# Re-pacing expert matmuls between the two halves of a macaron network, and rebuilding a state-space scan loop

## The chip, the cores and the metric

The kernel runs on one core of one Trainium2 chip. The metric is the device time of one execution in microseconds (us), the median of three runs. A core has TensorE (PE in the profile, with its weight loads as PEld), VectorE (DVE), ScalarE (ACT), GpSimd (POOL) and SyncE (SP); they run their own instruction streams and meet at semaphores.

## The reference

A batch of 8 sequences of 256 tokens, width 128, goes through four layers of the form "half a feed-forward, an attention, half a feed-forward", each on a layer-normed input. What matters here is layers 1 and 3:

```python
x = x + 0.5 * _L1_ffn_ref(_layernorm(x), ...)    # stage 3: 8 experts, a router, top 2
x = x + _L1_attn_ref(_layernorm(x), ...)         # stage 4: state-space scan, 16 states
x = x + 0.5 * _L1_ffn_ref(_layernorm(x), ...)    # stage 5
...
x = x + 0.5 * _L3_ffn_ref(_layernorm(x), ...)    # stages 9 and 11: attention, then 8 dense experts
x = x + _L3_attn_ref(_layernorm(x), ...)         # stage 10: selective scan, mlp, attention (gqa), mlp

# _L1_attn_ref, for each channel e and state n:
A = -exp(A_log);  a = exp(dt * A)
bt = where(abs(A) < 1e-5, dt, (a - 1) / (A + 1e-10))
h[t] = a[t-1] * h[t-1] + bt[t-1] * u[t-1]
y = sum over n of C[t, n] * h[t, n]
# _L1_ffn_ref
h = silu(xf @ gate_w + gate_b) * (xf @ up_w + up_b)
y = sum over the experts of probs[:, e] * (h @ down_w + down_b)
```

Stages 6 and 8 are a plain two-layer feed-forward (layer 2), stage 7 a chunked delta rule (l2_attn), and layer 0 (stages 0 to 2) an expert-choice mixture and an attention.

## The kernel before

All tokens go through stages 0 to 2. Then the tokens are split into two halves, a and b, of 4 sequences each (1024 tokens, 8 tiles of 128). Each half goes through stages 3 to 11; below "a7" is stage 7 of half a. Tokens lie on the partitions in the residual x; transposed copies (xnT) have the channels there.

`run` (L745) issues the stages in a written order: a3 a4 b3 b4 a5 a6 a7 b5 b6 b7 a8 a9 a10 b8 b9 b10 a11 b11. A scheduler then orders every engine's instructions; instructions issued earlier in the program go first where they are ready by its reckoning. So that the expert matmuls of one half fill the gaps of a dependent chain of the other, six pairs of stages are tied together by the dictionary `beside`: b3 to a4, a5 to b4, b5 to a7, a9 to b7, b9 to a10, a11 to b10. In the leading stage `step` (L790) notes certain matmuls: in l1_attn the two `cb` of each state (L996, 32 in all), in l2_attn the gram (L1117) and `ks` (L1188), in l3_attn the scan's `sc` (twice each, 64), the mlps' `ph` (8 each) and the `scT` of gqa (64). In the following stage `keep_pace` (L794) gives each expert matmul of fraction "part" of the stage an order-only dependency on the noted matmul at the same fraction of the list. It sets the place in TensorE's instruction stream and makes no semaphore wait.

The experts of l1_ffn (L822 to L914, stages 3 and 5) are 16 groups: 8 experts times two chunks of 512 tokens. A group has, for each of two blocks of 128 hidden units, `pg` (L895) and `pu` (L897), Silu on ScalarE (L899), the product on VectorE (L900), then `po` (L906), 8 matmuls of 128x128 into one PSUM tile, and four scalar_tensor_tensor on VectorE (L912), one for each tile of tokens, that add the tile times its router weight to x. The experts of l3_ffn (L1412 to L1438) are 16 groups as well: four `ph` (L1418), three activations and one VectorE operation into hT, 16 `po` (L1430), four scalar_tensor_tensor (L1436). Each float32 matmul stands in the profile as two records. An expert's weights come by a DMA into one of three buffers, issued by SyncE and ScalarE in turn.

l1_attn (L915 to L1011) has a prologue (norm, three projections `plow`, `pc`, `pdt` a chunk, softplus, causal convolution, Silu, and GpSimd copies that shift dt and u by one token), then a loop over 16 states. With all 1024 tokens of the half in a tile's free dimension, a state does:

- ScalarE: a = exp(A dt) (L983), th = tanh(A dt / 2) (L984), cu = dt u c2 (L985; c2 is 1 where |A| is tiny, else 0). exp and tanh of this loop, and the Silu of experts beside it, change the activation table.
- VectorE: th = (a + 1) th (L987), bu = th c1 us (L988)
- GpSimd: bu = bu + cu (L989)
- VectorE: four tensor_tensor_scan of 256 tokens, one for each sequence, with start value 0 (L992); then twice h = h cb (L997), where `cb` is C of this state spread over the partitions by a matmul (L996)
- TensorE: y += h, through the identity (L998)

The tiles at, bu, cu and h have two buffers each.

The steps of the prediction touch further: l2_attn's recurrence, 8 steps with VectorE, TensorE and GpSimd's diagonal products (`dg`, L1064, four a step); the batches of l3_scan (L1493): a convolution and transposes, eight `pbc` (L1564), eight steps of `sc` (L1570, one PSUM buffer), `gw` (L1576) and `y` (L1584), an output projection; l3_mlp (L1464) and l3_gqa (L1603).

## Time and profile before

| what | value |
|---|---|
| median of three runs | 3518.58 us (3516.72 to 3529.11) |
| the profiled execution | 3514.43 us |
| its span in the trace | 3512.2 us |
| mean TensorE clock granted | 0.815 of full speed |
| TensorE busy | 2757.2 us, 79% |
| VectorE, ScalarE, GpSimd busy | 51%, 28%, 14% |

The stages of the trace, in us from the start of the span, first instruction to last on any compute engine (a stage of one half overlaps its neighbour of the other):

| stages | from to |
|---|---|
| 0 to 2, all tokens | 0 to 963 |
| a3; a4 (its loop 1129 to 1262) | 963 to 1082; 1082 to 1268 |
| b3 (with and after a4) | to 1324 |
| b4 (its loop 1372 to 1507); a5 | 1324 to 1514; to 1570 |
| a6; a7 (its recurrence 1756 to 1816) | 1571 to 1600; 1571 to 1894 |
| b5; b6 | 1514 to 1889; 1891 to 1923 |
| b7; a8; a9 (experts from 2089) | 1889 to 2237; 1894 to 1957; 1957 to 2292 |
| b8; b9; a10 (scan, then gqa from about 2556) | to 2331; 2332 to 2805; 2303 to 2799 |
| a11 (experts from 2913); b10 (scan from 2845, gqa from about 3073) | 2800 to 3322; 2819 to 3315 |
| b11 | 3317 to 3508 |

How to read the profile: busy times are of one execution. A stage's limit is read from its own stretch, not from the totals: in some stretches TensorE is busy throughout, in others it waits for a chain of VectorE, ScalarE and GpSimd. A row of a table of stretches has the stretch, its length, then the busy time of PE, PEld, DVE, ACT and POOL with the number of instructions, the granted TensorE clock, and the DMA engines' share and rate. A row of groups has the line, engine, operation, tiles and shapes, how many, then busy us and the mean in ns, then the engine's idle time before them and what ended it.

### The profile page before, as it was taken

The page shows a single profiled execution, that of the slowest core. Times are in us where ns is not written, and L with a number is a line of the kernel's source. Part 1 is how long each engine was busy: PE and PEld are TensorE (multiplying, and loading weights), DVE is VectorE, ACT ScalarE, POOL GpSimd, SP SyncE. Part 2 cuts the span into 40 slices and gives each one's busy share as a digit, 9 for nine tenths or more (in the row PEclk, how much of TensorE's full clock was granted, in tenths as well). Part 3 has the DMA queues.
Part 4 walks back from the last instruction along what each step waited for, and adds up shares of the span by engine and source line. Part 5 has one row for each costly group of instructions (what it writes and reads, how often), then busy time and mean ns, then how long its engine had stood idle before and what let it go on. Part 6 is the DMA issues. An engine that isn't in the chain of part 4 may idle for free.

```text
span 3512.2 us, 38332 instructions
## 1 busy us (share of the span) xinstructions
PE 2757.2 (79%) x14748; PEld 1815.4 (52%) x14748; DVE 1798.2 (51%) x4474; ACT 993.2 (28%) x1497; POOL 505.9 (14%) x559
## 2 busy tenths in 40 slices
PE   5674687586396786797888888988959989849999
PEld 3463354355253342354664666655635556625666
DVE  5722454672346868766565655454463354443332
ACT  1010233101124625522233213342223332213322
POOL 0055110024201211301030112000020000120000
PEclk8587799668687987897788659988969969959969
DMA  5021433201200000011200300010021100110100
GB/s 196 7 32 26 109 85 116 82 20 23 56 23 3 10 28 3 9 32 49 76 7 15 102 12 13 19 41 1 21 67 28 50 3 7 34 51 26 35 12 25
DMA packets 103233, 136.18 MB, mean 39 GB/s; under 512 B 22933, under 2 KB 83546, under 8 KB 96922
## 3 DMA queue, kind: packets, MB, share of 16 engines
q1 hardware_dynamic: 67530, 85.61, 8.0%
q10 hardware_dynamic: 22848, 37.36, 3.4%
q0 software_dynamic: 12672, 10.76, 2.2%
q8 instruction: 116, 1.90, 0.2%
q14 instruction: 67, 0.55, 0.1%
HBM read 106.17 MB, written 27.53 MB: 38 GB/s over the span
## 4 chain that ended last, share of the span: by engine, by line
PE 46%; DVE 13%; ACT 4%; POOL 3%; issue 2%; DMA 1%; ACTq 0%; POOLq 0%; DVEq 0%; SPq 0%
PE ph L1418 6%; PE po L1430 6%; PE po L906 2%; PE fl L1136 2%; PE pbc L1564 2%; PE ctx L588 2%; DVE h L992 2%; POOL bu L989 2%; PE sc L1570 2%; PE pg L895 2%; PE pu L897 1%; PE y L1584 1%; PE tp L218 1%; PE po L1029 1%; PE sc L539 1%
## 5 line engine op out<-in xcount | busy, mean ns | idle before, releaser
L1430 PEld LDWEIGHTS po<-w_e,hT 128*128 128x128 f32 x2048 | 257.0, 193 | 73.6 <-issue 52.3
L1430 PE MATMUL po<-w_e,hT 128*128 128x128 f32 x2048 | 280.0, 281 | 7.9 <-DVE x_res L1436 4.2
L1418 PE MATMUL ph<-x2T,w_e 128*128 128x512 f32 x512 | 270.1, 632 | 10.0 <-ACT hT L1426 9.5
L1426 ACT ACTIVATE hT<-ph,w_l_cols 128x512 f32<-128x512 f32 x192 | 131.7, 687 | 292.2 <-PE ph L1418 291.6
L542 DVE TENSOR_REDUCE nm<-sc 128x3 f32<-128x384 f32 (+1 forms) x192 | 132.4, 690 | 150.5 <-PE sc L541 150.1
L906 PEld LDWEIGHTS po<-w_e,hT 128*128 128x128 f32 x1024 | 137.7, 203 | 99.9 <-DVE hT L900 51.2
L906 PE MATMUL po<-w_e,hT 128*128 128x128 f32 x1024 | 153.0, 295 | 28.6 <-DVE hT L900 15.3
L578 ACT ACTIVATE pr_e<-scT 128x384 f32<-128x384 f32 (+1 forms) x192 | 114.6, 597 | 192.6 <-PE scT L576 186.7
L218 PE MATMUL tp<-c_ident,xn 128*128 128x128 f32 x208 | 54.7, 399 | 144.3 <-DVE xn L238 137.9
L899 ACT ACTIVATE gs<-pg,w_l_bias 128x512 f32<-128x512 f32 x128 | 87.9, 687 | 263.4 <-PE pg L895 260.2
L998 PE MATMUL y<-h,c_ident 128*128 128x512 f32 x128 | 89.3, 836 | 89.2 <-DVE h L997 89.1
L895 PE MATMUL pg<-xnT,w_e 128*128 128x512 f32 x256 | 142.2, 639 | 9.0 <-ACT gs L899 9.0
L427 ACT ACTIVATE gs<-pg 128x512 f32<-128x512 f32 x64 | 38.2, 597 | 370.8 <-PE pg L422 370.8
L897 PE MATMUL pu<-xnT,w_e 128*128 128x512 f32 x256 | 140.8, 634 | 2.5 <-ACT gs L899 2.5
L432 PE MATMUL po<-w_l_wd,hT 128*128 128x128 f32 x512 | 84.4, 318 | 73.5 <-DVE hT L428 73.4
L1436 DVE SCALAR_TENSOR_TENSOR x_res<-po,gt,x_res 128x128 f32<-128x128 f32 x256 | 74.3, 347 | 120.6 <-PE po L1430 120.4
L912 DVE SCALAR_TENSOR_TENSOR x_res<-po,pr,x_res 128x128 f32<-128x128 f32 x256 | 75.0, 342 | 109.5 <-PE po L906 109.3
L539 PE MATMUL sc<-ks,qs 72*128 72x256 bf16 x256 | 79.8, 312 | 60.8 <-DVE nm L542 45.5
L1418 PEld LDWEIGHTS ph<-x2T,w_e 128*128 128x128 f32 x512 | 84.8, 197 | 81.2 <-ACT hT L1426 42.1
L440 POOL DMA_INDIRECT l_acc<-eo,idx x64 | 99.5, 1554 | 156.3 <-DMA l_acc<-eo,idx 67.2
L432 PEld LDWEIGHTS po<-w_l_wd,hT 128*128 128x128 f32 x512 | 76.7, 226 | 86.6 <-DVE hT L428 85.5
L588 PE MATMUL ctx<-pr_e,vz 128*32 128x256 f32 x512 | 116.9, 395 | 4.8 <-ACT pr_e L578 4.6
(578 smaller groups left out, 5934.2 us busy)
## 6 DMA issues: line engine op xcount, KB each, us to landing
l_parts<-sT SPq DMA_DIRECT2D x48, 192.0 KB
qs<-l_parts SPq DMA_DIRECT2D x16, 576.0 KB
w_l_wu<-in_l_wu ACTq DMA_DIRECT2D x8, 1024.0 KB
w_l_wg<-in_l_wg SPq DMA_DIRECT2D x8, 1024.0 KB
w_l_wd<-in_l_wd SPq DMA_DIRECT2D x8, 1024.0 KB
w_e<-in_l_e SPq DMA_DIRECT2D x16, 512.0 KB
w_e<-in_l_e ACTq DMA_DIRECT2D x16, 512.0 KB
w_e<-in_l_e ACTq DMA_DIRECT2D x16, 384.0 KB
```

The costliest lines, as they stand in the source:

```text
L432: nc.tensor.matmul(po[:, h, :], hT[:, k, h * P : (h + 1) * P], w["l0_wd"][:, e, k, :], start=(k == 0), stop=(k == 3),)
L440: nc.gpsimd.indirect_dma_start(out=acc[:, :], out_offset=bass.IndirectOffsetOnAxis(ap=idx[:, j : j + 1], axis=0), in_=eo[:, h, :], in_offs ...
L539: nc.tensor.matmul(sc[:, jj, 0:S], qs[0:72, h, 0:P], k, start=True, stop=False)
L542: nc.vector.tensor_reduce(blocks[:, hp * pr : hp * pr + hp, :], sc[:, :, 0:384].rearrange("p h (k t) -> p h k t", t=P), AX.X, ALU.max, neg ...
L578: nc.scalar.activation(pe, sc[:, :, 0:384], AF.Exp, scale=float(1.0 / np.sqrt(np.float32(8.0))))
L588: nc.tensor.matmul(o, z, pe[:, 0:S], start=(j == 0), stop=False)
L895: self.keep_pace(nc.tensor.matmul(pg, wg[:, c], xnT[:, cols], start=True, stop=True), (G * e + g) / (8 * G))
L897: self.keep_pace(nc.tensor.matmul(pu, wu[:, c], xnT[:, cols], start=True, stop=True), (G * e + g) / (8 * G))
L906: nc.tensor.matmul(po[:, i, :], hT[:, k, i * P : (i + 1) * P], wd[:, k * P : (k + 1) * P], start=(k == 0), stop=(k == 1),)
L1418: mm = nc.tensor.matmul(ps, we[:, k * P : (k + 1) * P], xnew[:, 512 * g : 512 * g + 512], start=True, stop=True)
L1426: nc.scalar.activation(hT[:, k, :], ps, AF.Relu, bias=bias)
L1430: nc.tensor.matmul(po[:, i, :], hT[:, k, i * P : (i + 1) * P], we[:, (4 + k) * P : (5 + k) * P], start=(k == 0), stop=(k == 3),)
```

## The change

There are four edits, in three places.

1. `beside` gets a stretch of the leading stage's list: the experts are spread over the fractions lo to hi of it. b3/a4, a5/b4 and a9/b7 keep 0 to 1; b5/a7 becomes 0 to 0.4, b9/a10 0 to 0.5, a11/b10 0.5 to 1.
2. l1_attn notes its two `pc` matmuls, in the prologue, four times each: 8 marks ahead of the 32 of the loop.
3. In l1_ffn the four scalar_tensor_tensor of a group become four ScalarE multiplications by the router weight into a new tile eo (two buffers) and one GpSimd addition of 128x512 into x.
4. In the scan loop the tile at holds two states, and the exponentials and tangents of two states are issued together; cu is made by a GpSimd tensor_scalar with one buffer in place of ScalarE; a GpSimd memset clears a at the first token of each sequence, and one recurrence over 1024 tokens takes the place of the four.

```diff
@@ run
-            beside = {(b, 3): (a, 4), (a, 5): (b, 4), (b, 5): (a, 7), (a, 9): (b, 7), (b, 9): (a, 10), (a, 11): (b, 10)}
+            beside = {
+                (b, 3): (a, 4, 0.0, 1.0), (a, 5): (b, 4, 0.0, 1.0), (b, 5): (a, 7, 0.0, 0.4), (a, 9): (b, 7, 0.0, 1.0),
+                (b, 9): (a, 10, 0.0, 0.5), (a, 11): (b, 10, 0.5, 1.0),
+            }
...
@@ keep_pace
-            mark = self.pace[int(part * len(self.pace))]
+            lo, hi, steps = self.pace
+            mark = steps[int((lo + (hi - lo) * part) * len(steps))]
@@ l1_ffn
+                    eo = wk.tile([P, 4, D], F32, name="eo", tag="eo")
                     for i in range(4):
-                        t = 4 * g + i
-                        nc.vector.scalar_tensor_tensor(
-                            self.x[:, t, :], po[:, i, :], pr[:, t, e : e + 1], self.x[:, t, :], ALU.mult, ALU.add
-                        )
+                        nc.scalar.mul(eo[:, i, :], po[:, i, :], pr[:, 4 * g + i, e : e + 1])
+                    xs = self.x[:, 4 * g : 4 * g + 4, :]
+                    nc.gpsimd.tensor_tensor(xs, xs, eo, ALU.add)
@@ l1_attn
-                    nc.tensor.matmul(ps, w["l1_in"][:, P + 64 : P + 80], xnT[:, c], start=True, stop=True)
+                    mm = nc.tensor.matmul(ps, w["l1_in"][:, P + 64 : P + 80], xnT[:, c], start=True, stop=True)
+                    self.step(mm, 4)
...
-                    at = wk.tile([P, 2, T], F32, name="at", tag="at")
-                    a, th = at[:, 0], at[:, 1]
-                    bu, cu, h = (wk.tile([P, T], F32, name=nm, tag=nm) for nm in ("bu", "cu", "h"))
-                    nc.scalar.activation(a, dts, AF.Exp, scale=A[:, n : n + 1])
-                    nc.scalar.activation(th, dts, AF.Tanh, scale=Ah[:, n : n + 1])
-                    nc.scalar.activation(cu, dtu, AF.Copy, scale=c2[:, n : n + 1])
+                    if n % 2 == 0:
+                        at = wk.tile([P, 2, 2, T], F32, name="at", tag="at")
+                        for i in range(2):
+                            nc.scalar.activation(at[:, i, 0], dts, AF.Exp, scale=A[:, n + i : n + i + 1])
+                            nc.scalar.activation(at[:, i, 1], dts, AF.Tanh, scale=Ah[:, n + i : n + i + 1])
+                    a, th = at[:, n % 2, 0], at[:, n % 2, 1]
+                    bu, h = (wk.tile([P, T], F32, name=nm, tag=nm) for nm in ("bu", "h"))
+                    cu = wk.tile([P, T], F32, name="cu", tag="cu", bufs=1)
+                    nc.gpsimd.tensor_scalar(cu, dtu, c2[:, n : n + 1], None, ALU.mult)
...
                     nc.gpsimd.tensor_tensor(bu, bu, cu, ALU.add)
-                    for b in range(self.B):
-                        s = slice(b * S, b * S + S)
-                        nc.vector.tensor_tensor_scan(h[:, s], a[:, s], bu[:, s], 0.0, ALU.mult, ALU.add)
+                    nc.gpsimd.memset(by_b(a)[:, :, 0:1], 0.0)
+                    nc.vector.tensor_tensor_scan(h, a, bu, 0.0, ALU.mult, ALU.add)
```

More of the change, by code (lines that the diff above doesn't have):

```diff
@@ L770, in run @@
                 if on(k):
-                    half.steps, half.pace = [], steps.get(beside.get((half, k)), [])
+                    other, stage, lo, hi = beside.get((half, k), (None, 0, 0, 0))
+                    half.steps, half.pace = [], None
+                    if (other, stage) in steps:
+                        half.pace = lo, hi, steps[other, stage]
                     half.stage(k)
@@ L787, in __init__ @@
         self.side, self.tag = ("left", "right")[k], "ab"[k]
-        self.steps, self.pace = [], []
+        self.steps, self.pace = [], None
     def step(self, inst, weight=1):
```

## The prediction

> **What bounds the kernel now.** I read the engine totals first, then the chain that ended last, then busy time by stage, then the scan loop instruction by instruction.

> ```profile
> PE 2757.2 (79%) x14748; PEld 1815.4 (52%) x14748; DVE 1798.2 (51%) x4474; ACT 993.2 (28%) x1497; POOL 505.9 (14%) x559
> ...
> PE 46%; DVE 13%; ACT 4%; POOL 3%; issue 2%; DMA 1%; ACTq 0%; POOLq 0%; DVEq 0%; SPq 0%
> ```

> TensorE is the common bound, but only 79% busy: the 21% is what re-pacing can win, if it lies where experts can be put. The table of stretches shows where (start and end, length, busy of PE, weight load, DVE, ACT, POOL, then the granted clock):

> ```profile
> 1129.00:1262.00 133.00, 98.91 (x215) 37.49 (x216) 107.37 (x147) 73.36 (x68) 41.65 (x16) 0.82 0.04 12
> 1262.00:1325.00 63.00, 62.96 (x311) 40.54 (x309) 38.50 (x103) 18.79 (x26) 0.00 (x0) 1.00 0.10 29
> ...
> 1816.00:1894.00 78.00, 52.25 (x161) 28.58 (x160) 54.19 (x102) 39.83 (x47) 2.16 (x2) 0.79 0.02 5
> ...
> 2556.00:2650.00 94.00, 57.22 (x314) 35.47 (x312) 51.21 (x128) 21.75 (x51) 21.96 (x61) 0.67 0.24 66
> ...
> 2990.00:3038.00 48.00, 47.32 (x303) 31.34 (x303) 21.48 (x41) 10.29 (x17) 3.21 (x3) 1.00 0.11 35
> ```

> Row 1 is half a's scan loop: TensorE idle a quarter, VectorE the longest. Row 2 is what b's experts of stage 3 have left after it: TensorE full. Row 3 is the end of a's l2_attn, row 4 the start of a's gqa (26 and 37 us idle). Row 5 is one of four batches of b's l3_scan with a's experts inside: TensorE full. The other loop, half b's (1372 to 1507), takes 135 us.

> Inside a scan loop VectorE and GpSimd take turns. Two places, each with what ran at the same moment (start, duration, engine):

> ```profile
> 1200.22 1.22 DVE L987 SCALAR_TENSOR_TENSOR at<-at 128x1024 f32<-128x1024 f32 x1
> ...
> 1203.44 2.35 POOL L989 TENSOR_TENSOR bu<-bu,cu 128x1024 f32<-128x1024 f32 x1 [6.78 <-ACT at L984]
> ...
> 1203.87 3.00 DVE L987 SCALAR_TENSOR_TENSOR at<-at 128x1024 f32<-128x1024 f32 x1
> ```

> The same instruction takes 1.22 us alone and 3.00 us when it starts 0.43 us into GpSimd's add: it ends 1.08 us after the add does, so it hardly ran beside it.

> [...] L997, one input in PSUM, keeps its 0.67. [...]a scan of 256 takes 0.71, four follow each other in 2.42. [...]

> **Part 1, the scan loop.** ScalarE's work (three 1.15 us activations a state and table loads) isn't the loop's limit; taking cu away and pairing exp and tanh frees it, and gains nothing by itself. What counts is the new GpSimd multiply: 128x1024 float32, one SBUF input, scalar per partition. No such operation is in the trace. Its neighbours are:

> ```profile
> L1108 POOL TENSOR_SCALAR bT<-bT 128x1024 f32<-128x1024 f32 x2 | 5.6, 2782 | 0.0
> ...
> L969 POOL COPY us<-u 128x1020 f32<-128x1020 f32 x2 | 2.1, 1034 | 251.9 <-ACT u L961 251.9
> ```

> I take 2.78, the same instruction with an immediate scalar, VectorE idle beside it; ends 1.03 (the copy) and 3.3 (softplus' blocked add, L704, 3.33). [...] 2.78 + 2.35 + L987 1.20 + L988 1.28 + the scan. The one scan costs 2.40 by the four's 2.42 less a little; the merge is worth almost nothing, and the memset (128x4; a 128x16 takes 153 ns) only writes and hides under other waits. Sum 10.0, with about 0.3 us of handovers 10.3 a state, 165 for 16 states, against 133 and 135: **+30 each, +60**. Queued behind the multiply on GpSimd is the same state's add, and behind that VectorE's scan; cu has one buffer, so multiply n+1 can start only after add n[...]. Ends: 1.03 gives 8.6 a state, +3 each; 3.3 gives +43 each; if the two engines ran freely together, VectorE's own 7.2 would give -17 each.

> **Part 2, stage 3 and 5 experts.** The order of the built instructions: before, 5 of 16 expert groups (one expert on 512 tokens) end beside the other half's l1_attn and 11 after it; changed, 3 stand in its prologue, 1 near its end, 12 after it, none in the loop. So the weighted pc marks pull experts ahead of the loop, into a place where TensorE is mostly idle. The 11 groups take row 2's 63 us at a full clock, 5.7 each; a twelfth is +5.7. Moving the combining step off VectorE (four of 0.34 us a group) to ScalarE (four of some 0.27, from the PSUM copy L659, at best) and one GpSimd add (1.04, the 128x512 of L1483) costs nothing under full TensorE: ScalarE's 2 x 0.69 + 4 x 0.3 = 2.6 of 5.7, and po, with its one buffer, is free after 1.2 us instead of 1.4. The experts' weight loads (one in three buffers, from SyncE's and ScalarE's queues in turn) move with the groups: a load has two experts, four groups or 23 us, of lead, and the DMA engines are 0.03 to 0.12 busy there, so I cost them at nothing; without that cover an expert would wait for its load at each e. The last group's chain gets some 1.5 longer, and three groups in the prologue with their Silu between the exponentials cost about 1 us of tables and queue. 5.7 + 1.5 + 1 = **+8 each, +16**; ends 0 and +14 each.

> **Part 3, a7 to a9.** In the new order b5's last groups stand before a7's end (before, three stood at its very end), so l2_ffn of b (b6, 24 us of TensorE) runs in row 3's 26 us of idle; a8 (27 us) goes behind b7's gram, into a stretch of 66 us with 17 idle, 9 of it usable. 24 + 9 = **-33**. a9's experts no longer go into b7's recurrence; its attention does (56 us of TensorE against about the same in experts before), so nothing else is won. Ends: 0, if a7's tail is held up by VectorE (54 of 78 busy), and -70, if most of the 121 us idle between 1571 and 2296 is filled.

> **Part 4, a10 with b9.** Before, eight expert groups were left for gqa and the mlp. Now 15 stand before 55% of a10's instructions, five of them in row 4's stretch: 5 x 7.3 = 36.5, just its 37 us idle. b10's norms then hide in a10's end, 6 us more: **-43**; ends -55 and -20.

> **Part 5, b10 with a11.** Groups now start at 0.5: after the scan. In the new order 8 of 16 stand beside b10's gqa and mlp, and 8 after b10's end. Beside the scan stand only a11's attention (batches 1 and 2) and nothing (3 and 4). Taking 8 groups out of row 5's kind of stretch looks like a gain of 58 us of TensorE. But a batch alone is a chain: convolution and transposes 8 us, 4 pbc 8, eight steps of sc 0.92, gw 0.96 and handovers at 2.2, the end 4: 38 us, TensorE busy 27 of it, at a lower clock (0.67 to 0.8 elsewhere at that busy share) some 46, against 48 now. So -4 for the two batches, the eight groups cost 8 x 7.3 = +58 after b10's end, the mlp is 7 shorter, b11's norms hide, 10: **+37**. If the lone scan goes at TensorE's pace: 0.

> **Sum.** +60 +16 -33 -43 +37 = +37. Against the profiled execution's 3514.4 (span 3512.2 and 2.2 around it) this is 3551; the median of the runs is 4.1 above that execution: **3555**.

> **Rivals.** R1, not slower: the GpSimd multiply is cheap, 1.03. The loop loses 3 each rather than 30, the sum becomes -17: 3502. It decides from 1.6 us down (37 over 32 states is 1.16 off 2.78). For it: the copy's row; against it: the same instruction type at 2.78. R2: b10's lone scan keeps TensorE's pace, part 5 is 0: 3519. [...] against it: sc has one buffer, and every step waits for gw. R3: GpSimd's queue. The new expert adds wait for ScalarE, which waits for TensorE, and l2_attn's diagonal products (L1064, 1.06 us, four of each 7.2 us step) stand behind them in order: two recurrences of 8 steps get one add (1.04) a step longer, +17, and b5's groups, held by the same queue, end as late as before, which takes half of part 3's gain, +17: 3589. For it: they share a queue; against it: few b5 groups stand in the recurrence. That the experts leave the scan loop instead of filling it is in the forecast already.

> **Chances.** Forecast 0.5, R1 0.2, R2 0.15, R3 0.15. A measurement of this kernel can tell about 0.5% from no change, 3501 to 3536. Half of R1 and the low end of part 3 are faster: 0.15. The rest of R1, R2 and a little of the forecast are same: 0.22. Slower: 0.63. Range 3497 (R1 and some of part 3's low end) to 3600 (R3, or a 3.3 us multiply).

> **What would show it.** In the loop: GpSimd's cu at 2.7 to 2.9 us, L987 and the scan lengthened or waiting for GpSimd, about 165 us a loop. 12 groups after each loop. b7's start near 1889 + 76 - 33. No idle stretch at gqa's start in a10. In b10 about 46 us for batches 3 and 4, and 58 us of experts alone between b10's end and b11. A multiply near 1 us, or batches of 35 us, would make the prediction wrong.

## The result, and the profile after

| | before | changed |
|---|---|---|
| median | 3519.32 us (4 runs, 3516.72 to 3529.11) | 3559.84 us (4 runs, 3551.65 to 3572.22) |
| ratio | | 1.0113, 95% interval 1.0073 to 1.0153 |
| span of the profiled execution | 3512.2 us | 3549.9 us |
| mean TensorE clock | 0.815 | 0.802 |

The change makes the kernel 1.1% slower. The forecast was 3555. The total is right and so is its sign; but the sum is right by luck: two of its terms are wrong by about 54 us in opposite directions, and that is the lesson of this case.

The engine totals of the changed kernel come first:

```profile
PE 2820.9 (79%) x14748; PEld 1845.6 (52%) x14748; DVE 1774.8 (50%) x4122; ACT 981.3 (28%) x1687; POOL 745.2 (21%) x687
```

TensorE issues the same 14748 records and is busy 64 us longer, at a mean clock of 0.802 where it was 0.815. So matmuls run slower somewhere: a hint at the clock that the totals before couldn't give. GpSimd is busy 239 us longer, with its waits inside instructions counted (4.88 us for a multiply of 2.65, below).

To find where the time went, I cut both traces at the same events: the last matmul of stage 2, of a5, of a9, the first `pv` of b10's scan, the last matmul of b11.

| section | before | changed | measured | forecast |
|---|---|---|---|---|
| up to the end of stage 2 (unchanged code) | 962.7 | 966.5 | +3.8 | 0 |
| stages 3 to 5 with both scans (parts 1, 2) | 606.8 | 628.6 | +21.8 | +76 |
| a6 to a9, b5 to b7 (part 3) | 721.4 | 741.2 | +19.8 | -33 |
| to b10's scan (part 4) | 554.8 | 504.0 | -50.8 | -43 |
| b10, a11, b11 (part 5) | 660.9 | 703.9 | +43.0 | +37 |
| sum | 3506.7 | 3544.3 | +37.6 | +37 |

The stretches of the changed kernel that answer to the rows shown of before (stretch, length, busy of PE, PEld, DVE, ACT and POOL, then the clock): a's scan loop, the experts after it, the end of a's l2_attn, the start of a's gqa, and batches 3 and 4 of b10's scan.

```profile
1130.00:1264.00 134.00, 111.13 (x126) 32.04 (x124) 115.93 (x80) 41.77 (x43) 120.12 (x49) 0.55 0.00 0
1264.00:1339.00 75.00, 75.00 (x347) 47.12 (x347) 29.40 (x59) 32.77 (x77) 15.31 (x12) 0.96 0.13 38
1838.00:1912.00 74.00, 48.01 (x182) 28.80 (x182) 53.92 (x125) 37.59 (x51) 3.43 (x3) 0.82 0.05 13
2600.00:2694.00 94.00, 84.23 (x513) 56.35 (x511) 57.82 (x147) 32.03 (x66) 21.46 (x60) 0.96 0.24 66
2934.00:3031.00 97.00, 69.41 (x406) 42.55 (x402) 34.64 (x53) 9.93 (x17) 5.02 (x4) 0.77 0.02 7
```

Row 1: the loop takes 134 us, not 165. GpSimd is busy 120 of them. TensorE has 126 records where it had 215 and yet is busy longer: with no experts in the loop the clock is 0.55, where it was 0.82 with them. Row 2: 12 groups after the loop and the rest of one that began in it, in 75 us. Row 3: a7's end has b6 in it and is 74 long, where it was 78. Row 4: the idle of gqa's start is filled, 84 of 94 busy where it was 57. Row 5: batches 3 and 4 without experts, with the 7 us ahead of them. From its first `pv` to its last matmul a batch takes 44.8 and 44.4 us; the same two took 43.6 and 44.8 before, with experts between (before's row of 48 us is wider than the batch in it).

**The scan loop.** Here is the part of its timeline that decides (start, duration, engine, line; in square brackets the idle time before):

```profile
1202.63 2.29 DVE L1004 TENSOR_TENSOR_SCAN h<-at,bu 128x1024 f32<-128x1024 f32 x1 [1.93 <-POOL bu L1001]
1202.69 4.88 POOL L997 TENSOR_SCALAR cu<-dtu,c 128x1024 f32<-128x1024 f32 x1
1204.84 2.07 DVE L999 SCALAR_TENSOR_TENSOR at<-at 128x1024 f32<-128x1024 f32 x1
...
1208.86 2.34 POOL L1001 TENSOR_TENSOR bu<-bu,cu 128x1024 f32<-128x1024 f32 x1 [1.24 <-DVE bu L1000]
1209.23 3.05 DVE L999 SCALAR_TENSOR_TENSOR at<-at 128x1024 f32<-128x1024 f32 x1
```

The multiply is recorded with 4.88 us, which looks like a disaster. But it starts just after the scan, waits for it until 1204.9, and then needs its 2.65. L999 starts at the same moment and takes 2.07, only 0.86 more than the 1.21 it takes alone: it ran **beside** most of the multiply. Against the two-input add, two lines down, it takes 3.05. So the add shuts VectorE out for nearly all its 2.34 us (0.37 had gone before L999 began, 1.84 it was delayed), the multiply for 0.86 of its 2.65.

**b7's recurrence.** Its first `ks` to its last took 54.5 us before and 103.5 after. Before, with a9's experts beside it:

```profile
2099.00:2120.00 21.00, 20.65 (x162) 18.38 (x161) 9.16 (x21) 2.59 (x5) 9.16 (x9) 1.00 0.01 2
2120.00:2140.00 20.00, 19.78 (x153) 17.44 (x153) 8.14 (x19) 2.86 (x6) 10.93 (x11) 1.00 0.10 27
2140.00:2158.00 18.00, 18.00 (x140) 16.07 (x140) 7.44 (x19) 2.77 (x7) 4.83 (x6) 1.00 0.01 1
```

And the same recurrence in the changed kernel, with a9's attention beside it:

```profile
2063.00:2090.00 27.00, 23.36 (x96) 21.60 (x96) 12.15 (x23) 3.74 (x9) 8.23 (x8) 0.50 0.00 1
2090.00:2118.00 28.00, 27.54 (x113) 24.92 (x112) 9.97 (x22) 2.69 (x8) 7.19 (x7) 0.50 0.00 1
2118.00:2146.00 28.00, 28.00 (x114) 25.01 (x113) 7.45 (x17) 1.27 (x4) 9.36 (x10) 0.50 0.00 1
2146.00:2173.00 27.00, 26.53 (x118) 25.10 (x117) 7.60 (x18) 1.78 (x5) 0.43 (x1) 0.50 0.00 1
```

In both TensorE is busy almost throughout. The clock column is what differs: 1.00 before, 0.50 changed. In 20 us it gets through 153 records before and about 80 after.

### The profile page after: what moved, and what is told of

It is laid out like the page before. It is cut to its first block, busy times and chain, and to the rows that moved or that the text cites. A ratio compares the mean times of both kernels' runs of the same rounds, so it can differ in the third digit from the quotient of the medians.

```text
span 3549.9 us, 38408 instructions
## 1 busy us (share of the span) xinstructions
PE 2820.9 (79%) x14748; PEld 1845.6 (52%) x14748; DVE 1774.8 (50%) x4122; ACT 981.3 (28%) x1687; POOL 745.2 (21%) x687
## 5 line engine op out<-in xcount | busy, mean ns | idle before, releaser
L1442 PE MATMUL po<-w_e,hT 128*128 128x128 f32 x2048 | 272.6, 280 | 7.9 <-DVE x_res L1424 4.6
L1430 PE MATMUL ph<-x2T,w_e 128*128 128x512 f32 x512 | 262.1, 617 | 9.2 <-ACT hT L1438 9.2
L908 DVE SCALAR_TENSOR_TENSOR hT<-pu,w_l_bias,gs 128x512 f32<-128x512 f32 x128 | 95.5, 746 | 165.6 <-PE pu L905 145.6
L914 PE MATMUL po<-w_e,hT 128*128 128x128 f32 x1024 | 147.5, 289 | 27.4 <-DVE sp L698 18.7
L1010 PE MATMUL y<-h,c_ident 128*128 128x512 f32 x128 | 115.0, 1026 | 55.1 <-DVE h L1009 55.1
L922 POOL TENSOR_TENSOR x_res<-x_res,eo 128x512 f32<-128x512 f32 x64 | 85.4, 1335 | 346.8 <-ACT eo L920 346.7
L997 POOL TENSOR_SCALAR cu<-dtu,c 128x1024 f32<-128x1024 f32 x32 | 155.2, 4851 | 4.1 <-DVE dtu L980 1.2
L218 PEld LDWEIGHTS tp<-c_ident,xn 128*128 128x128 f32 x208 | 35.5, 183 | 180.4 <-DVE xn L238 91.5
```

The lines of the kernel that those rows point to most:

```text
L914: nc.tensor.matmul(po[:, i, :], hT[:, k, i * P : (i + 1) * P], wd[:, k * P : (k + 1) * P], start=(k == 0), stop=(k == 1),)
L997: nc.gpsimd.tensor_scalar(cu, dtu, c2[:, n : n + 1], None, ALU.mult)
L1010: nc.tensor.matmul(y[:, s], self.ident, h[:, s], start=(n == 0), stop=(n == N - 1))
L1430: mm = nc.tensor.matmul(ps, we[:, k * P : (k + 1) * P], xnew[:, 512 * g : 512 * g + 512], start=True, stop=True)
L1442: nc.tensor.matmul(po[:, i, :], hT[:, k, i * P : (i + 1) * P], we[:, (4 + k) * P : (5 + k) * P], start=(k == 0), stop=(k == 3),)
```

## The experiments

A reader needs three columns for most of them: the time from stage 2's end to a5's end, from there to a9's end, and from there to the kernel's last matmul (before: 607, 721, 1216; changed: 629, 741, 1208). They are from one profiled execution each; the medians of before, measured alongside, were 3516.8 to 3518.9.

| kernel | median | ratio to before, 95% interval | sections |
|---|---|---|---|
| scan_alone | 3551.5 | 1.0120 (1.0064 to 1.0175) | 646, 722, 1210 |
| combine_alone | 3522.5 | 1.0021 (1.0003 to 1.0038) | 617, 712, 1220 |
| places_alone | 3516.4 | 0.9995 (0.9973 to 1.0017) | 575, 761, 1210 |
| cu_copy | 3552.1 | 1.0119 (1.0064 to 1.0174) | 622, 741, 1208 |
| cu_act | 3539.6 | 1.0071 (1.0047 to 1.0095) | 614, 749, 1210 |
| b5_full | 3536.3 | 1.0058 (1.0039 to 1.0077) | 631, 726, 1210 |
| a11_full | 3496.2 | 0.9942 (0.9922 to 0.9963) | 629, 745, 1149 |
| hold_attn | 3583.3 | one run | 631, 776, 1201 |
| dense_fill | 3533.8 | one run | 628, 750, 1189 |
| best1 | 3423.9 | 0.9735 (0.9710 to 0.9759) | 574, 732, 1164 |

### Each part alone

scan_alone is before.py with edit 4 (at, cu, memset, one recurrence) and nothing else.

> The kernel before with the scan edit alone (two states a tile, cu as a GpSimd tensor_scalar, one recurrence). In the built order 2 of 16 expert groups stand beside l1_attn, 14 after it (before: 5 and 11). Theory A (the forecast: the multiply shuts VectorE out for its whole 2.78 us): each loop 165 us instead of 133, and 3 more groups of 5.7 after it: 3519 + 60 + 34 = about 3613. Theory B (the multiply shuts VectorE out for under 1 us of it): each loop stays at 134, so only the groups count: 3519 + 34 + 2 = about 3555.

3551.5: theory B. Its loops are 134.2 and 132.5 us long (first L987 to the end of the last scan), before 132.0 and 134.1. All of its loss lies in the groups that follow each loop, 14 instead of 11: the loop is as long as before, but in the scheduler's order it has been emptied of experts. So the rewritten loop isn't free either: in before's first loop the experts held VectorE for 9.4 us (L900, L912), in this one's for 1.5, and the loop got no shorter by that.

places_alone has edits 1 and 2 (the stretches and the marks) and nothing else.

> The kernel before with the new stretches and the pc marks alone (scan and combining step as before). In the built order 9 of 16 groups stand beside l1_attn. If the old scan loop can carry 7 groups at little cost, 4 groups of 5.7 fewer follow each loop: -40 or so; the rest as in the changed kernel's trace: +18 in a7 to a9, -51 in a10, +43 in b10 and b11. Together 3519 - 40 + 10 = about 3490. If the loop grows by what it takes in (its VectorE is 107 of 133 us busy), about 3530.

The first section is 32 us shorter: the old loops take in 6 to 7 groups each, where they had 3 to 4, and get only 5 us (1130.8 to 1267.6) and 2 us longer. The late section is as expected. But a6 to a9 cost 40, not 18, so the whole comes out at zero where I expected -27. b7's recurrence takes 103 us, as in the changed kernel; the further 20 us lie ahead of a7's recurrence (9) and between b7's gram and its recurrence (10), and aren't explained.

combine_alone has edit 3 and nothing else.

> The kernel before with the combining step alone on ScalarE and GpSimd. Stages 3 to 5 end TensorE-bound as before, so nothing there. Theory E (rival R3 of the prediction, seen in b5_full's trace, where a7's recurrence with b5's groups in it took 74 us instead of 60): the GpSimd adds stand in one queue with the recurrence's diagonal products, +13 in a7's recurrence and none in b7's, which has l3 experts: 3517 + 13 = 3530. Without such a queue: 3517.

3522.5, and a7's recurrence takes 60 us as before. Theory E, and rival R3 of the prediction with it, fall: the GpSimd adds don't hold the recurrence. The edit isn't neutral everywhere: its loops take 138 us each, 6 and 4 more than before, and its second section is 9 shorter. What slowed a7's recurrence in b5_full is seen below.

### The multiply in the loop

cu_copy, on the changed kernel:

```diff
-                    nc.gpsimd.tensor_scalar(cu, dtu, c2[:, n : n + 1], None, ALU.mult)
+                    nc.gpsimd.tensor_copy(cu, dtu)
```

> The changed kernel with cu made by a GpSimd copy of dtu (the factor c2 is left out of the computation). A copy of this size took 1.03 us before. Theory A: each of 32 states gets 1.75 us shorter, 3560 - 56 = about 3504. Theory B: the copy shuts VectorE out about as long as the multiply does, and only every second state, in which the add waited for cu, gets 0.6 shorter: 3550 to 3560, the loops 129 to 134 us.

3552.1, loops of 130.0 and 128.9 us (134.0 and 132.9 in the changed kernel): theory B. Here is the copy, behind the scan as the multiply was:

```profile
1210.07 2.29 DVE L1004 TENSOR_TENSOR_SCAN h<-at,bu 128x1024 f32<-128x1024 f32 x1 [1.35 <-POOL bu L1001]
1210.09 3.09 POOL L997 COPY cu<-dtu 128x1024 f32<-128x1024 f32 x1
1212.27 1.99 DVE L999 SCALAR_TENSOR_TENSOR at<-at 128x1024 f32<-128x1024 f32 x1
```

The copy takes 0.8 us once the scan is over and delays L999 by 0.78, about as much as the multiply of 2.65 (0.86). How long a GpSimd instruction runs and how long it shuts VectorE out are two numbers. What sets the second isn't separated: the copy reads one input and shuts VectorE out for nearly all its time, the multiply reads one and doesn't.

cu_act takes the multiply off GpSimd again:

```diff
-                    nc.gpsimd.tensor_scalar(cu, dtu, c2[:, n : n + 1], None, ALU.mult)
+                    nc.scalar.activation(cu, dtu, AF.Copy, scale=c2[:, n : n + 1])
```

> The changed kernel with cu back on ScalarE (one buffer, otherwise as changed); the built order of the experts is the changed kernel's. Theory B (the multiply shuts VectorE out for about 0.86 us of its 2.7): each state gets that much shorter, 32 x 0.86 = 28: loops of 120 instead of 134 us, 3560 - 28 = about 3532. If the multiply costs the loop nothing at all: loops of 134 and 3560.

3539.6, between the two; neither expectation holds. The loops are 129 us, 4 to 5 shorter each, not 14. The trace shows where most of the rest went. L1009 is the product with `cb`, first in the changed kernel's loop, then in this one's:

```profile
L1009 DVE TENSOR_TENSOR h<-h,cb 128x512 f32<-128x512 f32 x30 | 19.7, 675 | 0.8 <-PE cb L1008 0.8
...
L1009 DVE TENSOR_TENSOR h<-h,cb 128x512 f32<-128x512 f32 x30 | 20.1, 679 | 13.8 <-PE cb L1008 13.8
```

VectorE's wait for GpSimd's add fell from 17.3 us to 6.4, but now it waits 13.8 us for TensorE, at a mean clock of 0.58 in a loop without experts. The total is weak evidence: the profiled execution, 3550.9, is one of the two longest of seven, and of the 15 us that its first section wins the second loses 8; what of the 15 lies outside the loops isn't explained.

### b7's recurrence and the clock

b5_full changes one number of the changed kernel, b5's stretch of a7, back to 0 to 1.

> The changed kernel with b5's experts again over all of a7, so that a9's experts again stand in b7's recurrence and a9's attention ahead of it. Theory C (the recurrence took 110 instead of 59 us in the changed kernel because it has a9's attention in it in place of experts, and TensorE's clock is 0.55): recurrence back at about 60 us, b7 starts later again by about 40, a9 ends some 18 us earlier: 3542. Rival D (it is slow because GpSimd's queue or the new combining step holds it): recurrence stays above 100 us and the later start adds to it: 3580 or more.

3536.3: theory C. b7's recurrence takes 54.5 us again. But a7's takes 73.6, which neither theory had. Its steps take 18.9, 14.1, 10.7 and then 7.1 to 7.7, and its eight `ks` 1.9, 1.75, 1.75 and then 0.98 us. At a clock of 0.50, in the changed kernel's b7, eight `ks` take 1.75: the start of a7's recurrence has that length too. best1 shows the clock itself there, 0.50, without the combining step (below). The kernel before has a slow start for one step only (`ks` of 1.9 us, a step of 14.9 at a mean clock of 0.60, from the next one on 1.00).

hold_attn and dense_fill ask whether it is the clock or the work in between. Both keep a9's attention out of b7's recurrence; dense_fill adds work.

```diff
# hold_attn: a9's first matmuls, in the order only, behind a late ks of b7
-                        nc.tensor.matmul(ps, w["l3_in"][:, j * P : (j + 1) * P], xnT[:, c], start=True, stop=True)
+                        mm = nc.tensor.matmul(ps, w["l3_in"][:, j * P : (j + 1) * P], xnT[:, c], start=True, stop=True)
+                        if self.pace and self.pace[0] == 0.0 and self.pace[1] == 1.0:
+                            self.keep_pace(mm, 0.999)
# dense_fill: behind ks, in each step of half b
+                        if self.tag == "b":
+                            fill = psum.tile([P, 512], F32, name="fill", tag="fill")
+                            for _ in range(3):
+                                nc.tensor.matmul(fill, self.ident, kd.rearrange("p b s -> p (b s)"), start=True, stop=True)
```

> The changed kernel with a9's attention held, in the order of TensorE's instructions, behind the seventh step of b7's recurrence, so that the first six or seven steps run with nothing between them. Theory F (TensorE's clock is low where it has only small matmuls, and the recurrence goes at that clock): the clock stays under 0.65 and a step takes 9 us or more, against 7.2 with experts beside it. Theory G (the steps are slow since a9's attention stands between them in order and waits): a step takes 7.2 us or less.

> The changed kernel with three extra matmuls of 128x512 in each step of b7's recurrence (their result is not used; a9's attention falls behind the recurrence in the built order, as in hold_attn). That is 2.8 us of TensorE a step at full clock. Theory F: they raise the clock to 0.85 or more, the step's own matmuls get faster, ks 1.2 us instead of 1.75, and a step takes no longer than in hold_attn, 7 to 9 us. Theory G: the clock stays and a step gets 3 to 5 us longer than in hold_attn.

Inside the recurrence of hold_attn, which has only its own matmuls of 32 columns:

```profile
2080.00:2105.00 25.00, 21.05 (x94) 20.39 (x94) 5.46 (x11) 0.53 (x2) 8.24 (x8) 0.50 0.00 1
2105.00:2130.00 25.00, 20.72 (x93) 19.92 (x92) 5.16 (x11) 0.80 (x3) 11.12 (x11) 0.50 0.00 1
```

And of dense_fill:

```profile
2020.00:2040.00 20.00, 19.06 (x121) 14.40 (x119) 7.22 (x14) 0.53 (x2) 14.08 (x13) 0.99 0.01 2
2040.00:2060.00 20.00, 20.00 (x128) 15.15 (x128) 5.27 (x15) 0.80 (x3) 12.23 (x12) 1.00 0.00 1
```

A step takes 11.0 us alone, and **7.1 us with three more matmuls in it**, whose result nobody uses; `ks` goes from 1.88 to 0.97. The first step of dense_fill takes 12.8, then the clock is at 0.99 to 1.00. Theory F's numbers hold in both runs: 0.50 and 11.0 us a step without the added matmuls, 0.99 to 1.00 and 7.1 with them. G has a share: with a9's attention in between, at the same 0.50, a step took 14.1 instead of 11.0. So of the 7 us that a step of the changed kernel lost, 4 are the clock's effect on the bare step and 3 the attention that stands in line at that clock. With the dead work the kernel takes 3533.8 us, against 3583.3 in hold_attn (one run each); 26 us of that lie between a5's end and a9's. Against the changed kernel's 3559.8 it is no proof: there the same stretch is 9 us shorter (741 against 750), since its attention needn't wait behind the recurrence, and what dense_fill gains lies after a9 and isn't explained. The rows of both runs show two values, 0.50 and 0.99 to 1.00; what sets them isn't shown. The changed kernel's row with 28.00 busy of 28.00 us stood at 0.50, before's with 18.00 of 18.00 at 1.00: a busy column near 100% doesn't tell which one it is.

### The end, and the best version

a11_full changes one number of the changed kernel, a11's stretch of b10, back to 0 to 1.

> The changed kernel with a11's experts over all of b10, as before the change; in the built order 8 of their groups stand beside b10's scan and 8 beside its gqa and mlp, none after b10. Theory H (the prediction's part 5: the lone scan gains almost nothing from having no experts in it, so the 8 groups after b10 are pure loss): 44 us shorter, as in best1, where a9's end to the kernel's end is 1164 us against the changed kernel's 1208: 3516. Rival (R2: the scan without experts runs at TensorE's pace): the scan gets longer again by 36 or more, and the total stays within 10 us of 3560.

3496.2, with the late section 59 us shorter: theory H, and more than expected. b10's batches 3 and 4 take 44.8 and 44.4 us in the changed kernel with nothing beside them (2941.3 to 2986.1, 2986.6 to 3031.0) and 42.1 and 44.5 in a11_full with experts between. What the experts cost there is nothing; taken out, they cost their full time after b10.

best1 keeps the two numbers that paid, on the kernel before: the pc marks, and b9 over 0 to 0.5 of a10.

```diff
...
+            beside = {
+                (b, 3): (a, 4, 0.0, 1.0), (a, 5): (b, 4, 0.0, 1.0), (b, 5): (a, 7, 0.0, 1.0), (a, 9): (b, 7, 0.0, 1.0),
+                (b, 9): (a, 10, 0.0, 0.5), (a, 11): (b, 10, 0.0, 1.0),
+            }
...
+                    self.step(mm, 4)
```

> The kernel before with the pc marks and b9 over the first half of a10, and nothing else of the change. From places_alone: stages 3 to 5 are 32 us shorter; a7 to a9 as before, 0; b10's start moves 51 us ahead by b9's new stretch, and a11's experts beside b10 as before keep it: 3517 - 32 - 51 = about 3435. Rival: the late gain is given back, as in the changed kernel, where a9's end to the kernel's end was 1208 us against 1216: 3480.

3423.9, 2.65% faster than before, and better than expected: -32, +10 and -51 in its sections. The +10 is a7's recurrence (73 us instead of 60), whose start is at a clock of 0.50 until b5's experts are in it, at 1.00 from 1760 on:

```profile
1713.00:1735.00 22.00, 21.09 (x74) 16.45 (x74) 7.27 (x11) 1.64 (x3) 13.14 (x13) 0.50 0.14 38
1735.00:1760.00 25.00, 25.00 (x122) 19.91 (x121) 8.05 (x20) 2.59 (x5) 8.20 (x8) 0.68 0.03 7
1760.00:1790.00 30.00, 29.65 (x220) 25.46 (x219) 13.30 (x34) 5.30 (x10) 11.61 (x12) 1.00 0.02 9
```

This profiled execution, 3437.8 us, was the longest of best1's four runs; it and the profiled one of before are 77 us apart, 73 of them in these sections, where the medians are 95 apart.

## Why the prediction was right, and where it was wrong

- **Part 1, +60: wrong, measured +1.** The failing step is the sum 2.78 + 2.35 + 1.20 + 1.28 and the scan: it sets the multiply, the add and the three VectorE instructions one behind the other, as if VectorE stood still for all of each GpSimd instruction. The duration was right (2.6 to 2.7 once it is let in). But the profile of before showed the standstill for the add alone (L987 3.00 us against 1.22); for the multiply it was the author's estimate. The runs show a delay of 0.86 us, and 2.35 + 0.86 + 1.20 + 1.28 + 2.29 = 8.0, which leaves 0.4 for handovers in the trace's 8.4 (two states in turn, 9.6 and 7.3 from scan to scan). Rival R1 had the right loop for a wrong reason: it wanted a multiply of 1.03 us. Two ends of this part don't come out of its own numbers: 3.3 us makes about +39 each, not +43, and L987, L988, the scan and two L997 make 6.2 us a state, not 7.2. The forecast doesn't rest on them.
- **Part 2, +16: right, measured +21.** 12 groups after each loop, as the order told, 9 and 7 us for the twelfth and the longer chain, 4 in the second prologue.
- **Part 3, -33: wrong, measured +20.** b7 did start earlier: its gram began 22 us sooner, its recurrence 36 (62, counted from a5's end). The failing step is "its attention does (56 us of TensorE against about the same in experts before), so nothing else is won". Equal TensorE time isn't equal work: the 54.5 us of recurrence became 103.5, since with the attention's matmuls (8 to 256 columns) the clock was 0.50, where with the experts' (128 and 512) it was 1.00. Counted from a5's end: 62 sooner, 49 longer in the recurrence, 33 longer in what follows it, where a9's experts now stand. Without the 49 the part would have been -29. The clock column stood in the profile of before: 1.00 in b7's recurrence, 0.57 in the stretches ahead of it with the attention (1996 to 2089). I read it as a price, not as something that the move would change.
- **Part 4, -43: the size was right, measured -51, the place was not.** gqa's start was filled, but its own chain takes as long as before (from the last batch of the scan to the first `sc` of gqa 80 us before, 85 after). The gain is later: gqa and the mlp without experts in them (15 us), and b10's preparation, which hides in a10's end (10 us from there to b10's first `pv` instead of 49, where the forecast had 6 us of gain).
- **Part 5, +37: right, measured +43.** A batch alone took 45 us where 46 was worked out, though the 48 that it was set against was 44 to 45, the scan 191 against 193, 8 groups (58 us) after b10's end. R2 falls, by a11_full.
- **R3**: falls, by combine_alone.

The errors are -54 on the stages 3 to 5 (+22 for +76) and +53 on a7 to a9 (+20 for -33). A total that fits isn't a check on its terms; only the cut by sections was.

Two things stay open. Why the scheduler takes the experts out of the loop once the scan is rewritten was read from the order, and not looked into; it decides edit 4's loss, since the loop itself is as long as before. And what exactly raises the clock, matmul width or the pauses between, wasn't separated: with three added matmuls of 512 columns a step it was 0.99 to 1.00, with the attention's matmuls of up to 256 it was 0.50.

## What to carry to other kernels

Filler for a dependent chain on TensorE is to be chosen by what it does to the clock, not only by its length: with expert matmuls between them the steps of this chain took 7 to 8 us at a clock of 1.00, with an attention's in their place 14 at 0.50. Before a stage is moved beside another, read the clock column of both places, and look for what held it up. And check a forecast by sections between the same events in both traces; the sum can be right by two errors.
